# A mixture-of-experts layer and a LoRA layer on one core: the same work in a newly searched order

## The chip, the cores and the metric

The kernel runs on one core of a Trainium2 chip. A core has a matrix engine (TensorE, PE in the profile; its weight loads are PEld), three engines for elementwise work (VectorE or DVE, ScalarE or ACT, GpSimd or POOL) and SyncE (SP), which here only issues DMAs. Each engine works through its own queue in order, and they wait for each other by semaphores. The metric is the device time of one execution in microseconds (us), median of several runs.

## The reference

The input `x` is 2 batch rows x 1024 tokens x 256 channels; `cond_8` (2 x 8) holds the router's logits and also the LoRA weights. Cut to what is computed:

```python
rw = softmax(router_logits); w, sel = top_k(rw, 2); w = w / w.sum()
mlp(x, g, u, d) = (gelu(x @ g) * (x @ u)) @ d          # 256 -> 1024 -> 256
x = x + sum(w[k] * mlp(x, expert sel[k])) + mlp(x, shared)
x = x + x @ W_base.T + b_base + 2.0 * sum_e cond[b, e] * Bs[e] @ (As[e] @ x)
```

The router picks per batch row, so each row runs one shared and two chosen experts. The second line is computed as one matrix per batch row, `W_base` plus the mixed LoRA product.

## The kernel before, in words

**Tiling.** The tokens of a batch row are two tiles `t` of 512, the channels two blocks `c` of 128. Work on the experts goes in 24 *groups* `g` = (batch row, shared or chosen expert 1 or 2, quarter of the 1024 hidden units), 12 per batch row. Every f32 operand is kept as two parts: `hi`, a rounded copy (`hi_of`, a cast by ScalarE, L179), and `lo`, the rest (`lo_of`, a subtraction by VectorE or GpSimd, L182). A product is three matmuls: hi x hi, lo x hi, hi x lo of weights and x, in this order (L289), so the low half of x is wanted by the third.

**A group.** Groups 1 to 23 compute the 2 x 2 block product (hidden half `i`, token tile `j`) with seven products instead of eight, by sums of weight blocks (`weight_sum`, S1 to S4, on GpSimd, L221) and of x blocks (`x_sum`, L261 to L267). They are named P1 to P7, with g or u behind for the gate or the up half: P1, P6, P7 and P4 go into PSUM banks `ps_ag`/`ps_au`, P2, P5 and P3 into `ps_dg`/`ps_du`. On the way ScalarE copies a bank out (`keep`: r1 after P1, u2 after P6, u3 after P7, L316) and VectorE adds the copy to the d bank (`add_part`, named "r1 added u" and so on, L322). Then for each block `ij`: `gelu ij` on ScalarE (L331), `act ij` = `times_up` on VectorE (gelu times up times gate weight, L337/L339), `act_hi` (ScalarE) and `act_lo` (VectorE), and two halves of `down` on TensorE (L361) into four banks `y[j][c]`, which add up over the 12 groups of a batch row. A name with 10 behind it, as `times_up 10`, means block i = 1, j = 0; block 10 reads `ps_ag`/`ps_au` directly, so the next group's P1 has to wait for `gelu 10` and `times_up 10`. Group 0 is computed plainly with eight products (`plain_product`, L311), the first of them in two halves of 256 tokens, as its inputs are just arriving; its block products are called "product ij of k" (k is the half of the 256 channels).

**Order.** There is no scheduler at run time: the program hands each piece of work to `at(t, f, ...)` with a planned time in units of one TensorE product of 0.68 us (`LEN = 22` units a group), the list is sorted by that time, and a dependency chain fixes this order on every engine. Pieces that come in each group get the time `g * LEN + REGULAR[name]` by `reg`. `MOVED` shifts single pieces, named by their place in the list, against their time. So a planned time sets only the order in each queue; what waits at run time is decided by data and buffers. Names in the table: "A hi/A1 lo/A2 lo" split the weight blocks of the next group, "S hi/S lo" the sums, "D hi/D0 lo/D1 lo" the down weights, "load" fetches the weights of the group after next: from HBM by SP for the shared expert, by an indirect DMA on GpSimd's queue for the chosen ones.

**Start, batch change and end.** SP issues the first loads in pieces; 27 small matmuls warm TensorE up. The router runs in group 1 or so (`router`, seven VectorE operations; `gate_exp` and `gelu_table` on ScalarE switch its function table twice). At the end of batch row 0, `finish_y` (L406) adds `y` to the old x and so frees the four `y` banks for the next row's `down`; `split_xa` splits the sum for the second layer, whose two LoRA matrices were made in groups 4 and 5 (`weff_*`). The second layer of row 0 runs beside the other row's end, then that of row 1.

Of the kernel before, what the change touches and what calls it, by code (L numbers as in the profile page):

```python
# [53 lines left out]
SCALING = 2.0  # L54
PIECE = 2
REGULAR = {
    "P1g": -3.9, "P2g": -1.8, "P1u": -0.9, "S1": -0.9, "r1g": -0.8, "A hi": -0.3, "r1 added g": 0.9,
    "r1u": 1.1, "P6g": 2.7, "u2g": 2.7, "P6u": 4.6, "P2u": 5.0, "u2u": 6.0, "S2": 6.7, "P7g": 7.3, "S4": 7.3,
    "P5g": 7.6, "S3": 7.7, "A1 lo": 7.8, "load": 7.9, "u3g": 8.5, "P5g mix": 9.6, "P7u": 10.6,
    "r1 added u": 12.2, "P5u": 12.7, "P4g": 13.2, "u3 added g": 13.3, "gelu 00": 14.1, "act 00": 14.1,  # L60
    "u3u": 14.2, "S hi": 14.8, "P3g": 15.5, "P4u": 15.7, "S lo": 16.0, "gelu 11": 16.0, "gelu 10": 16.1,
    "hi 00": 17.0, "u3 added u": 17.8, "act 11": 18.0, "P3u": 18.1, "u2 added g": 18.1, "act 10": 18.4,
    "hi 11": 18.8, "down 00 0": 19.7, "u2 added u": 20.8, "gelu 01": 20.8, "lo 00": 21.2, "act 01": 23.3,
    "hi 10": 25.6, "lo 10": 25.6, "lo 11": 25.7, "down 00 1": 26.2, "hi 01": 28.6, "down 10 0": 29.0,
    "down 10 1": 31.1, "lo 01": 31.6, "A2 lo": 31.6, "D hi": 34.0, "down 11 0": 34.2, "down 11 1": 34.2,
    "down 01 0": 34.3, "D1 lo": 34.3, "down 01 1": 34.5, "D0 lo": 36.4,
}
MOVED = {
    33: -4.6, 40: 6.9, 59: -0.5, 75: -1.5, 87: -22.6, 100: 1.7, 101: 3.2, 190: 0.2, 1587: 10.8, 1599: 5.5,
    1605: 5.0,  # L70
}
WARM = 27
LEN = 22
# [15 lines left out]
def moe_then_lora(ctx: ExitStack, tc: tile.TileContext, x, cond, skill, shared, piece0, second, outT):  # L89
# [16 lines left out]
    def at(t, f, *args):  # L106
        plan.append((round(t + MOVED.get(len(plan), 0), 1), len(plan), f, args))
# [210 lines left out]
    sums, ge, act, acts = {}, {}, {}, {}  # L318
# [49 lines left out]
    mix, bias_sb = lin[:, (2 + NC) * C:(2 + NC) * C + B], lin[:, (2 + NC) * C + B:]  # L368
# [77 lines left out]
    V, A, G = nc.vector, nc.scalar, nc.gpsimd  # L446
# [50 lines left out]
    for n, ij in enumerate(((0, 0), (1, 0), (0, 1), (1, 1))):  # L497
        t = (6, 8, 10, 16)[n]
# [72 lines left out]
    for g, b in MIX_AT.items():  # L571
        t0 = g * LEN
# [23 lines left out]
    for b in range(B):  # L596
        t0 = (b + 1) * (1 + TOP_K) * NPC * LEN
# [3 lines left out]
    for b in range(B - 1):  # L601
        t0 = (b + 1) * (1 + TOP_K) * NPC * LEN
        for t in range(T):
            for c in range(NC):
                at(t0 + (10.2, 14.2)[t] + c / 10, finish_y, b, t, c)
                at(t0 + (t + 1) * LEN + 8 + 8 * c, split_xa, b, t, c, hi_of, A)
                at(t0 + (t + 1) * LEN + 9 + 8 * c, split_xa, b, t, c, lo_of, V)


    t0, tt = NG * LEN, (NG - 1) * LEN  # L610
    b = B - 1
# [96 lines left out]
```

## Time and profile before

| what | us |
|---|---|
| median of 3 runs (lowest, highest) | 383.69 (383.64, 384.94) |
| the profiled execution's own time | 383.77 |
| its span, first to last instruction | 382.0 |
| TensorE busy | 377.4 |
| VectorE busy | 307.5 |
| ScalarE busy | 255.6 |
| GpSimd busy | 207.6 |
| granted TensorE clock | 1.000 |

Matmuls are pipelined, so that each is shown longer (0.39) than the distance to the next (0.23); lost time on TensorE is best read from starts, not from busy time. In a row of the timeline the columns are start, length, engine, line, operation, what it writes and reads, count of merged instructions, and in brackets the engine's idle time before it with what ended it. A VectorE operation's recorded length overlaps the next one's start by about 0.08.

### The profile page before, as it was taken

The page shows a single profiled execution, that of the slowest core. Times are in us where ns is not written, and L with a number is a line of the kernel's source. Part 1 is how long each engine was busy: PE and PEld are TensorE (multiplying, and loading weights), DVE is VectorE, ACT ScalarE, POOL GpSimd, SP SyncE. Part 2 cuts the span into 40 slices and gives each one's busy share as a digit, 9 for nine tenths or more (in the row PEclk, how much of TensorE's full clock was granted, in tenths as well). Part 3 has the DMA queues.
Part 4 walks back from the last instruction along what each step waited for, and adds up shares of the span by engine and source line. Part 5 has one row for each costly group of instructions (what it writes and reads, how often), then busy time and mean ns, then how long its engine had stood idle before and what let it go on. Part 6 is the DMA issues. An engine that isn't in the chain of part 4 may idle for free.

```text
span 382.0 us, 4888 instructions
## 1 busy us (share of the span) xinstructions
PE 377.4 (99%) x1695; PEld 312.4 (82%) x1695; DVE 307.5 (81%) x423; ACT 255.6 (67%) x439; POOL 207.6 (54%) x215
## 2 busy tenths in 40 slices
PE   9999999999999999999999999999999999999996
PEld 8788788888888888888888888888888888888885
DVE  5999978678787889988798897777778778777686
ACT  3878876776666866867767777667666667665520
POOL 0587777777565574553454655755555556550100
PEclk9999999999999999999999999999999999999999
DMA  8711220220211204041250112012022021000014
GB/s 232 275 46 55 85 82 1 84 82 0 84 29 53 86 5 160 2 137 36 103 192 1 45 41 82 9 75 82 2 82 82 2 84 54 28 2 0 0 57 165
DMA packets 8215, 26.00 MB, mean 68 GB/s; under 512 B 1024, under 2 KB 2304, under 8 KB 8192
## 3 DMA queue, kind: packets, MB, share of 16 engines
q0 software_dynamic: 2304, 12.58, 10.6%
q1 hardware_dynamic: 5888, 13.12, 10.0%
q8 instruction: 13, 0.21, 0.2%
q14 instruction: 10, 0.08, 0.1%
HBM read 23.60 MB, written 2.10 MB: 67 GB/s over the span
## 4 chain that ended last, share of the span: by engine, by line
PE 96%; DMA 1%; DVE 1%; SPq 1%; ACT 0%; issue 0%
PE y L361 34%; PE ps_au L289 17%; PE ps_ag L289 17%; PE ps_dg L289 13%; PE ps_du L289 13%; DMA w_raw<-in_piece 1%; SPq L255 0%; PE ps_dg L384 0%; PE ps_dg L311 0%; PE ps_du L311 0%; SPq L209 0%; DVE wd L182 0%; ACT acts L179 0%; DVE act L337 0%; DVE xr L263 0%
## 5 line engine op out<-in xcount | busy, mean ns | idle before, releaser
L361 PE MATMUL y<-acts,wd 128*128 128x512 f32 x576 | 150.1, 390 | 0.4 <-ACT acts L179 0.4
L361 PEld LDWEIGHTS y<-acts,wd 128*128 128x128 f32 x576 | 107.8, 188 | 23.3 <-ACT acts L179 0.8
L182 DVE TENSOR_TENSOR acts<-act,acts 128x512 fp32r<-128x512 f32 x96 | 76.2, 820 | 14.2 <-ACT acts L179 13.7
L182 POOL TENSOR_TENSOR wa<-w_raw,wa 128x512 fp32r<-128x512 f32 (+1 forms) x46 | 56.1, 1224 | 30.4 <-ACT wa L179 24.0
L182 POOL TENSOR_TENSOR wd<-w_raw,wd 128x256 fp32r<-128x256 f32 x44 | 37.2, 863 | 53.6 <-ACT wd L179 53.5
L221 POOL TENSOR_TENSOR sf<-w_raw 128x256 f32<-128x256 f32 x46 | 37.3, 811 | 49.9 <-DVE ws L182 38.9
L179 ACT CAST acts<-act 128x512 fp32r<-128x512 f32 x96 | 58.0, 620 | 4.7 <-DVE act L337 2.8
L339 DVE SCALAR_TENSOR_TENSOR act<-ge,gate_w,c_u 128x512 f32<-128x512 f32 x48 | 46.5, 970 | 3.0 <-ACT ge L331 0.5
L331 ACT ACTIVATE ge<-c_g 128x512 f32<-128x512 f32 x69 | 43.7, 633 | 0.4
L331 ACT ACTIVATE ge<-ps_ag 128x512 f32<-128x512 f32 x24 | 14.4, 601 | 43.6 <-PE ps_ag L289 43.6
L322 DVE TENSOR_TENSOR c_u<-ps_du,u_u 128x512 f32<-128x512 f32 x46 | 31.6, 686 | 12.0 <-PE ps_du L289 12.0
L182 DVE TENSOR_TENSOR ws<-sf,ws 128x1024 fp32r<-128x1024 f32 (+1 forms) x24 | 28.2, 1179 | 14.7 <-ACT ws L179 14.7
L316 ACT COPY u_g<-ps_ag 128x512 f32<-128x512 f32 x46 | 27.1, 589 | 18.4 <-PE ps_ag L289 16.4
L289 PE MATMUL ps_au<-x,ws 128*128 128x512 f32 x138 | 38.9, 390 | 0.0
L289 PE MATMUL ps_ag<-x,ws 128*128 128x512 f32 x138 | 38.8, 389 | 0.0
L289 PE MATMUL ps_au<-x,wa 128*128 128x512 f32 x138 | 38.8, 389 | 0.0
L289 PE MATMUL ps_ag<-x,wa 128*128 128x512 f32 x138 | 38.7, 389 | 0.0
L289 PE MATMUL ps_du<-x,ws 128*128 128x512 f32 x138 | 38.7, 389 | 0.0
L289 PE MATMUL ps_dg<-x,ws 128*128 128x512 f32 x138 | 38.7, 389 | 0.0
L316 ACT COPY u_u<-ps_au 128x512 f32<-128x512 f32 x46 | 27.0, 588 | 13.4 <-PE ps_au L289 13.4
L322 DVE TENSOR_TENSOR c_g<-ps_dg,u_g 128x512 f32<-128x512 f32 x46 | 31.3, 680 | 5.1 <-PE ps_dg L289 4.7
L289 PEld LDWEIGHTS ps_au<-x,ws 128*128 128x128 f32 x138 | 25.8, 188 | 5.7 <-ACT u_u L316 0.4
(105 smaller groups left out, 554.6 us busy)
## 6 DMA issues: line engine op xcount, KB each, us to landing
w_raw<-in_shared SPq DMA_DIRECT2D x7, 768.0 KB, 4.5
xr<-in_x SPq DMA_DIRECT2D x15, 256.0 KB, 3.6
lora_in<-in_second SPq DMA_DIRECT2D x1, 514.0 KB, 6.1
w_raw<-in_piece SPq DMA_DIRECT2D x4, 128.0 KB, 2.7
outT<-sf SPq DMA_DIRECT2D x1, 512.0 KB, 2.8
outT<-u_g SPq DMA_DIRECT2D x2, 256.0 KB, 2.0
outT<-u_u SPq DMA_DIRECT2D x2, 256.0 KB, 2.0
outT<-ge SPq DMA_DIRECT2D x4, 128.0 KB, 1.7
```

Of the source, the lines that this page charges most:

```text
L179: (eng.copy if eng is nc.scalar else eng.tensor_copy)(pair[:, 0, :], src)
L182: eng.tensor_tensor(pair[:, 1, :], src, pair[:, 0, :].bitcast(F32), ALU.subtract)
L221: eng.tensor_tensor(ssum(i), a, b, op)
L289: nc.tensor.matmul(ps, lhsT=l, rhs=r, start=(start and n == 0), stop=(n == len(parts) - 1), skip_group_check=True)
L316: nc.scalar.copy(part[m, h], bank["a", h])
L322: nc.vector.tensor_tensor(sums[g, h, ij], bank["d", h], part[m, h], ALU.add)
L331: nc.scalar.activation(ge[g, ij], result(g, 0, ij), AF.Gelu_apprx_tanh)
L339: nc.vector.scalar_tensor_tensor(act[g, ij], ge[g, ij], gate_w[:, s - 1, b:b + 1], result(g, 1, ij), ALU.mult, ALU.mult)
L361: nc.tensor.matmul(y[j][c], lhsT=w[:, wp, o:o + P], rhs=a[:, ap, :], start=first and n == 0, stop=last and n == 2, skip_group_check=True)
```

## The change

No instruction is added or taken away; only the planned times are others, and so the order in the queues. Three places change: the table of regular times, the list of moved pieces (11 before, 52 after), and the planned times of `finish_y` for the first batch row. Most of the moved pieces lie in groups 0 to 6 (places 24 to 410). Among them: place 24 is the low split of P2's x block of group 0, 33 an `x_sum`, 37 `gate_weights`, 59 and 78 the `gelu 10` and the `act_lo 11` of group 0, 87 to 101 the sums and their splits for groups 1 and 2, 110 to 198 products, keeps and loads of groups 1 and 2, 1539 the split of the first LoRA matrix, 1557 and 1559 splits of the second batch row's x, 1599 and 1605 splits at the end.

```diff
 REGULAR = {
-    "P1g": -3.9, "P2g": -1.8, "P1u": -0.9, "S1": -0.9, "r1g": -0.8, "A hi": -0.3, "r1 added g": 0.9,
-    "r1u": 1.1, "P6g": 2.7, "u2g": 2.7, "P6u": 4.6, "P2u": 5.0, "u2u": 6.0, "S2": 6.7, "P7g": 7.3, "S4": 7.3,
-    "P5g": 7.6, "S3": 7.7, "A1 lo": 7.8, "load": 7.9, "u3g": 8.5, "P5g mix": 9.6, "P7u": 10.6,
-    "r1 added u": 12.2, "P5u": 12.7, "P4g": 13.2, "u3 added g": 13.3, "gelu 00": 14.1, "act 00": 14.1,
...
-    "hi 10": 25.6, "lo 10": 25.6, "lo 11": 25.7, "down 00 1": 26.2, "hi 01": 28.6, "down 10 0": 29.0,
-    "down 10 1": 31.1, "lo 01": 31.6, "A2 lo": 31.6, "D hi": 34.0, "down 11 0": 34.2, "down 11 1": 34.2,
-    "down 01 0": 34.3, "D1 lo": 34.3, "down 01 1": 34.5, "D0 lo": 36.4,
+    "P1g": -3.7, "S1": -1.3, "r1g": -0.3, "P2g": 0.0, "S2": 0.8, "P1u": 1.2, "A hi": 1.4, "P6g": 1.6,
+    "r1 added g": 1.9, "r1u": 2.2, "load": 3.4, "u2g": 3.8, "S4": 3.8, "P6u": 4.6, "P2u": 5.0, "P7g": 6.5,
+    "u2u": 6.6, "S3": 7.0, "P5g": 7.2, "u3g": 7.2, "gelu 00": 9.7, "P5g mix": 10.1, "r1 added u": 10.3,
+    "P7u": 10.5, "S hi": 10.6, "u3 added g": 11.6, "P5u": 12.0, "A1 lo": 12.1, "u3u": 12.9, "act 00": 13.5,
...
+    "down 00 1": 24.5, "hi 10": 26.0, "lo 11": 28.2, "lo 10": 28.4, "hi 01": 28.7, "down 11 0": 29.4,
+    "down 10 0": 30.1, "D hi": 30.4, "lo 01": 30.8, "A2 lo": 32.5, "down 11 1": 33.6, "D1 lo": 37.8,
+    "down 10 1": 38.6, "down 01 0": 39.1, "D0 lo": 39.2, "down 01 1": 40.1,
 }
 MOVED = {
-    33: -4.6, 40: 6.9, 59: -0.5, 75: -1.5, 87: -22.6, 100: 1.7, 101: 3.2, 190: 0.2, 1587: 10.8, 1599: 5.5,
-    1605: 5.0,
+    24: 3.3, 33: -9.8, 37: 3.8, 45: 3.7, 59: -1.6, 78: 3.8, 87: -35.7, 92: 2.9, 97: 8.9, 99: 6.7, 100: 6.7,
+    101: 5.2, 107: -4.6, 110: -2.1, 111: -0.7, 115: -1.7, 120: -0.9, 121: -3.7, 124: 2.7, 128: -2.9,
...
+    347: -4.2, 349: 4.4, 350: -4.6, 351: 2.5, 355: -8.3, 407: 6.8, 410: -6.4, 780: -0.9, 1539: 7.4,
+    1557: 5.4, 1559: 2.4, 1599: 1.6, 1605: 1.9,
 }
...
-                at(t0 + (10.2, 14.2)[t] + c / 10, finish_y, b, t, c)
+                at(t0 + (16.8, 18.4)[t] + c / 10, finish_y, b, t, c)
```

## The prediction

> **What bounds the kernel now.** I read the busy shares first, then the table by stage, then the chain of waits, and only then single instructions where the chain leaves TensorE.
>
> The page's first two parts (engine, busy time and share; then tenths in 40 slices):
>
> ```profile
> PE 377.4 (99%) x1695; PEld 312.4 (82%) x1695; DVE 307.5 (81%) x423; ACT 255.6 (67%) x439; POOL 207.6 (54%) x215
> PE   9999999999999999999999999999999999999996
> PEclk9999999999999999999999999999999999999999
> ```
>
> TensorE has work in every slice but the last and its clock is full. The busy time of single stretches (start:end, length, then each engine's busy time) says where it isn't:
>
> ```profile
> 0.00:17.00 17.00, 15.81 (x86) 13.10 (x87) 12.01 (x23) 8.79 (x17) 4.50 (x10) 1.00 0.84 277
> 17.00:41.00 24.00, 24.00 (x106) 19.39 (x105) 22.20 (x37) 20.63 (x37) 19.12 (x18) 1.00 0.18 50
> 41.00:189.00 148.00, 148.00 (x660) 122.69 (x659) 122.35 (x161) 105.80 (x182) 93.53 (x96) 1.00 0.20 66
> ```
>
> From 41 us on TensorE is busy every moment. The chain in order of time (start, length, what) shows the pace; one group is what lies between two of these rows:
>
> ```profile
> 101.56 2.72 PE y L361 x12
> ...
> 116.52 2.72 PE y L361 x12
> ...
> 131.48 2.72 PE y L361 x12
> ```
>
> 2.72/12 = 0.2267 us a matmul, 14.96 us = 66 x 0.2267 a group: no slot is lost. No order can shorten that; it can only lose. What an order can win are the slots lost before 41 us. TensorE's instructions in order of time there:
>
> ```profile
> 10.98 1.52 PE L311 MATMUL y<-x,wa 128*128 128x512 f32 x6
> 12.85 1.77 PE L361 MATMUL y<-acts,wd 128*128 128x512 f32 x6 [0.36 <-ACT acts L179]
> 14.46 0.39 PE L311 MATMUL ps_dg<-x,ws 128*128 128x512 f32 x1
> ...
> 18.59 0.94 PE L289 MATMUL ps_dg<-x,wa 128*128 128x512 f32 x3
> 19.37 0.86 PE L361 MATMUL y<-acts,wd 128*128 128x512 f32 x3
> ...
> 38.44 0.84 PE L361 MATMUL y<-acts,wd 128*128 128x512 f32 x3
> 39.21 0.96 PE L289 MATMUL ps_au<-x,ws 128*128 128x512 f32 x3
> 40.01 1.32 PE L361 MATMUL y<-acts,wd 128*128 128x512 f32 x5
> ```
>
> Starts against starts: from 10.98 to 14.46 are 3.48 us for 12 slots of 0.2267 (2.72), so 0.76 lost: group 0's first `down`, which waits for its activations. 18.59 to 19.37 is 0.78 for three slots (0.68): 0.10, P2g of group 1 behind `gelu 11`. 38.44 to 40.01 is 1.57 for six (1.36): 0.21, P7u of group 2 behind `keep u2 u`. With about 0.15 at the first matmul (3.88) that is 1.2 us, all there is to win; the span cannot fall below 382.0 - 1.2 = 380.8, a time of 382.6.
>
> **Outside the change.** SP's queue is in the same order in both kernels, TensorE's first 13 products too, ScalarE's work up to about 17 us, and the tail's products from 362 us (there only the lo splits of the last group and of the last sums change places). So the 3.88 us ahead of the first matmul and the 4.3 us after the last stay: 0.
>
> **Part 1: P2's low half three places later on VectorE (the loads assumed late).** VectorE's rows:
>
> ```profile
> 7.29 0.42 DVE L179 CAST x<-xr 128x512 fp32r<-128x512 f32 x1
> 7.75 0.69 DVE L182 TENSOR_TENSOR x<-xr,x 128x512 fp32r<-128x512 f32 x1
> 8.72 0.43 DVE L182 TENSOR_TENSOR wa<-w_raw,wa 128x256 fp32r<-128x256 f32 x1 [0.27 <-ACT wa L179]
> 9.06 0.68 DVE L263 TENSOR_TENSOR xr<-xr,xr 128x512 f32<-128x512 f32 x1
> 9.66 0.69 DVE L261 TENSOR_TENSOR xr<-xr,xr 128x512 f32<-128x512 f32 x1
> ```
>
> The 7.75 row is P2's low half. In the new order the L263 sum takes its place (to about 8.40), the wa split still starts at 8.72 (it waits for ScalarE, whose cast waits for its load), and P2's low half starts at 9.06 and ends at 9.75. L261 then starts at 9.66 as before: the rest of VectorE's chain (P3, wd, `times_up 00` at 11.47) keeps its times. But TensorE's product 00 of k=1 reads that half in its fifth matmul, at 9.16; it now waits to 9.75 + 0.05 = 9.80 (0.05 is what the `down` at 12.85 took after its cast ended at 12.80). Loss: 0.64. `gelu 00` starts at 10.59 when ScalarE is free, and the accumulation now ends at 9.80 + 0.23 + 0.39 = 10.42: no delay; `gelu 10` moves from 11.08 to about 11.6 and ends before ScalarE's next cast at 12.18. So TensorE arrives at `down 00` at 12.34 + 0.64 = 12.98, after the activations' hi half (12.85); its fifth matmul comes at 12.98 + 0.91 = 13.89, just as the lo half is there (13.16 + 0.68 + 0.05). It ends at 14.34 where it was 14.46. The wait of 0.76 has changed places with one of 0.64: net -0.12.
>
> A rule that would make it dearer: the Trainium skill (VectorE: DVE Perf Modes, The DRAIN you can't avoid) says that the next Vector operation does not start until the pipe is empty; its next section lets an instruction that is not held start earlier. Here 9.06 starts 0.09 before 8.72 + 0.43. By the drain rule P2's low half would end at 9.15 + 0.69 = 9.84, a loss of 0.73 and a net of -0.03. I take the rows.
>
> **Part 2: groups 0 to 2.** P6's low half moves up into VectorE's idle 0.69 us before `act_lo 10` (15.13): 14.36 to 15.05, cost nothing. Against this stands the Trainium skill (GPSIMD Engine Reference, 1. Specifications): GpSimd shares its SBUF interfaces with Vector instructions of two SBUF inputs. GpSimd works from 13.40 to 15.00, and the sum at 12.07, beside GpSimd, took 1.17. At that price `act_lo 10` slips by 0.4; TensorE reads it at about 19.2, nearly 3 us after its end, so the sum stays. P2g goes two products later (about 20.5), `gelu 11` ends about 19.7: the 0.10 goes. In group 2 `keep r1 u` follows a P1u that sits one product later, but `act_hi 10` now stands ahead of the table switch and not behind it: P1u ends about 34.3, the keep 34.95; two table loads (1.28 each) and two 0.20 operations end about 37.9; `keep u2 u` 38.4, P7u wants it at 38.9: the 0.21 goes, with 0.45 to spare. The router's seven operations (2.0 us, 22.64 to 24.66 now) pass `act_lo 11`, which then ends about 25.2; its `down` wants it at 26.9. P5u of group 1 moves two products later and wants `r1 added u` (26.4) at 28.0. Narrowest is `times_up 10` of group 1: at the stretched durations it ends about 33.0, and P1u of group 2, moved one product later, wants it at 33.5. New waits here: 0 to 0.5, taken as 0.05, since all stand at zero with the rows' own durations.
>
> **Part 3: the regular times.** TensorE's products are the same; two other engines' reads of its banks change. The tightest wait every group has is P6u on `keep r1 u` (it ends at 200.79, P6u starts at 201.36: 0.57), and it is untouched. The others, counted in products of 0.68 between a bank's writer and its next use: from P6g to P7g there were five and are four, so P7g's margin on `keep u2 g` goes from 1.93 to 1.25. From P2u to P5u there were ten and are seven, 2.04 less, of which VectorE gives back some, as `r1 added u` also moves up: from about 3.6 to 2.1; in groups 13 and 14, where the second layer's splits stand on VectorE, 0.8. From P4g to the next group's P1u there were seven and are ten: the margin on `times_up 10` grows from 1.7 to about 3. GpSimd's load of two groups ahead is issued 4.5 units (3 us) earlier, ahead of S4 and S3: those come 1.3 us later, some 8 us ahead of their reader. Nothing: 0. If a stretched Vector operation (0.5 more, 12.07 against 9.66) meets a narrow group, 0.5 each; not in all.
>
> **Part 4: the sums at the batch change.** Now:
>
> ```profile
> 190.45 1.29 DVE L406 TENSOR_TENSOR xa<-y,xr 128x512 f32<-128x512 f32 x2 [1.34 <-PE y L361]
> 193.85 0.69 DVE L406 TENSOR_TENSOR xa<-y,xr 128x512 f32<-128x512 f32 x1 [0.32 <-PE y L361]
> ```
>
> All four move behind the last `down` of group 11, which itself is later. That ends about 197.3; two sums of 0.69 (0.60 apart) run to 198.6; behind them on VectorE stands `times_up 10` of group 12 (0.68), to 199.2, and P1u of group 13 needs it at about 199.3 (TensorE now: 199.32). Margin near 0.1; taken as 0.05, at most 0.5, with `act_lo 00` behind it still 0.3 early.
>
> **Sum.** -0.12 - 0.10 - 0.21 + 0.05 + 0.05 = -0.33 on the profiled execution's 383.77 (span 382.0 and 1.77 around it): 383.44. That execution is 0.08 above the median of 383.69, so on the median it is 383.36. I say 383.4.
>
> **Rivals.** (a) The old waits go but new ones of the same size come, in group 1 and at the batch change (0.5 + 0.5 at their upper ends, less what is counted): 383.4 + 0.4 to 0.9, so 383.8 to 384.3. For it: VectorE is busy 22.2 of 24 us between 17 and 41. Against: each wait has a margin at the measured durations. (b) Slower than before by one mechanism: P2's low half is late and `down 00` doesn't absorb it, because its activations slip as far. Place: product 00, k=1, at 9.16; price 0.64 + 0.12 back: 383.4 + 0.76 = 384.2. It decides as soon as L261 starts over 0.4 us after 9.66. Against: the wa split, the load behind it, and P2's low half end where that chain began before. (c) A regular wait in every group: P5u's margin of 2.1 is used up. From 0.1 us in each of 22 groups: 385.6 and more. For it: one operation stretches by 0.5; against: it takes four or five in a row. (d) The change does nothing that counts: 383.7.
>
> **Numbers.** Chances: forecast 0.55 (own range 383.0 to 383.8), (d) 0.12, (a) 0.15, (b) 0.08, (c) 0.08, all idle gone with luck 0.02. Half a per cent, about what a measurement of this kernel can tell from no change, is 1.9 us; below 381.8 lies under the 382.6 that TensorE's work allows. Hence faster 0.02, same 0.90, slower 0.08. Range 382.8 to 384.8, from the floor to past (a) and (b).
>
> **What would show it.** TensorE's fifth matmul of product 00, k=1, starting at 9.8; no wait left at `down 00`, P2g of group 1 or P7u of group 2; the spacing of 14.96 kept; P1u of group 13 with at most 0.2 lost. A spacing above 15.0, or a wait over 1 us anywhere after 17 us, would make it wrong.

## The result and the profile after

| | before | after |
|---|---|---|
| median, us (lowest to highest, runs) | 383.86 (383.60 to 384.94, 22) | 384.87 (384.35 to 385.70, 22) |
| ratio to before, 95% interval | | 1.0021, 1.0015 to 1.0027 |
| the profiled execution's own time | 383.77 | 385.22 |
| its span | 382.0 | 383.4 |
| VectorE busy | 307.5 | 317.4 |

The changed kernel is slower by 0.21% (0.15 to 0.27%), some 0.8 us (the two medians lie 1.0 apart); that is within the half per cent that was called no change. Forecast was 0.3 us less than before, so the sign is wrong, and the time lies just outside the range.

The page's first part, and then the busy time of single stretches (start:end, length, then PE, PEld, DVE, ACT and POOL with their counts, granted clock, DMA share, GB/s), both of the kernel after:

```profile
PE 377.6 (98%) x1695; PEld 312.3 (81%) x1695; DVE 317.4 (83%) x423; ACT 254.4 (66%) x439; POOL 204.4 (53%) x215
```

```profile
0.00:17.00 17.00, 15.10 (x84) 12.75 (x85) 12.07 (x23) 8.71 (x16) 3.97 (x9) 1.00 0.80 268
17.00:41.00 24.00, 24.00 (x108) 19.77 (x107) 20.31 (x36) 21.05 (x38) 18.20 (x18) 1.00 0.26 85
41.00:189.00 148.00, 147.43 (x656) 121.70 (x655) 129.60 (x162) 104.24 (x182) 95.19 (x97) 1.00 0.18 61
189.00:205.00 16.00, 16.00 (x72) 13.19 (x71) 14.23 (x21) 10.83 (x20) 6.93 (x8) 1.00 0.34 116
205.00:355.00 150.00, 150.00 (x664) 124.19 (x663) 121.58 (x156) 101.51 (x175) 78.18 (x83) 1.00 0.13 43
```

Three things are to be seen. From 205 to 355 us, some ten groups, TensorE is busy every moment, and its starts there keep the pace of 0.2267 us without a loss: the new regular times cost nothing in each group. Around the batch change (189 to 205) it is full too. But between 41 and 189, where it was full before, 0.57 us are missing, and VectorE took 129.6 us where it took 122.4, for one operation more. So VectorE's operations became longer there, not more.

Read as in the prediction (starts against starts), TensorE's lost slots are these, in us, each with the 0.11 or so that the matmul after a wait comes late as well:

| place | before | after |
|---|---|---|
| the first product, from 3.88 to 5.51 us | 0.27 | 0.27 |
| product 00 of k=1, on P2's low half | 0 | 1.33 |
| first `down` 00 of group 0 | 0.74 | 0 |
| P2g of group 1, P7u of group 2 | 0.29 | 0 |
| P2g of group 3 | 0 | 0.11 |
| **P5g of group 4** | 0 | **0.85** |
| `down` 11 of group 23 | 0 | 0.11 |
| second layer at the end | 0.15 | 0.15 |
| sum | 1.45 | 2.82 |

The difference is 1.37; the spans differ by 1.44, the rest being remnants below 0.04 each. The start has 0.6 of it, and P5g of group 4 has 0.85; the small waits gone (0.29) and come (0.22) nearly cancel. The timeline of after shows what happened at the start:

```profile
8.86 0.41 ACT L183 CAST wa<-w_raw 128x256 fp32r<-128x256 f32 x1 [2.54 <-DMA w_raw<-in_piece]
...
9.30 0.43 DVE L186 TENSOR_TENSOR wa<-w_raw,wa 128x256 fp32r<-128x256 f32 x1 [1.12 <-ACT wa L183]
...
9.64 0.68 DVE L186 TENSOR_TENSOR x<-xr,x 128x512 fp32r<-128x512 f32 x1
...
10.38 0.50 PE L315 MATMUL ps_ag<-x,wa 128*128 128x512 f32 x1 [1.06 <-DVE x L186]
...
13.69 1.52 PE L365 MATMUL y<-acts,wd 128*128 128x512 f32 x6
```

In this execution the fourth weight piece landed 0.58 us later than in the one of before (ScalarE's cast, 8.86 against 8.28), and everything behind it moved by as much: the `wa` split from 8.72 to 9.30, P2's low half to 9.64, the matmul to 10.38. `down` 00 (13.69) no longer waits.

The other part is P5g of group 4. The same view of after, 64 to 71 us:

```profile
64.31 0.75 POOL L225 TENSOR_TENSOR sf<-w_raw,sf 128x256 f32<-128x256 f32 x1
64.39 3.84 DVE L341 TENSOR_TENSOR act<-ge,c_u 128x512 f32<-128x512 f32 x1
...
65.01 0.73 POOL L186 TENSOR_TENSOR wa<-w_raw,wa 128x256 fp32r<-128x256 f32 x1
...
65.70 0.73 POOL L225 TENSOR_TENSOR sf<-w_raw 128x256 f32<-128x256 f32 x1
...
66.40 1.28 POOL L186 TENSOR_TENSOR wa<-w_raw,wa 128x512 fp32r<-128x512 f32 x1
...
68.27 0.62 ACT L183 CAST acts<-act 128x512 fp32r<-128x512 f32 x1 [1.25 <-DVE act L341]
68.79 0.58 ACT L320 COPY u_g<-ps_ag 128x512 f32<-128x512 f32 x1
69.28 0.62 ACT L183 CAST wd<-w_raw 128x512 fp32r<-128x512 f32 x1
69.79 0.59 ACT L393 COPY wef<-ps_dg 128x512 f32<-128x512 f32 x1
...
70.43 0.96 PE L293 MATMUL ps_dg<-x,ws 128*128 128x512 f32 x3 [0.57 <-ACT wef L393]
```

From below upwards: P5g needs the bank `ps_dg`, out of which ScalarE must first copy the LoRA product (`weff_keep`, L393). That copy is the third in ScalarE's queue behind a cast of `act` (68.27), for which ScalarE stood idle for 1.25 us. The `act` is VectorE's `times_up 01` of group 3, and that took 3.84 us where such an operation, with no GpSimd beside it, takes 0.68. While it lasted, GpSimd worked through four operations without a break (64.31 to 67.68): S4, the A2 split of group 4, S3 and the A1 split of group 5. `times_up` ended 0.55 after the last of them. In the kernel before, the same pieces lay far apart:

```profile
60.20 1.07 POOL L221 TENSOR_TENSOR sf<-w_raw,sf 128x256 f32<-128x256 f32 x1
61.22 0.74 POOL L221 TENSOR_TENSOR sf<-w_raw 128x256 f32<-128x256 f32 x1
...
63.41 1.29 POOL L182 TENSOR_TENSOR wa<-w_raw,wa 128x512 fp32r<-128x512 f32 x1 [1.44 <-ACT wa L179]
...
64.05 1.20 DVE L337 TENSOR_TENSOR act<-ge,c_u 128x512 f32<-128x512 f32 x1
...
69.42 0.73 POOL L182 TENSOR_TENSOR wa<-w_raw,wa 128x256 fp32r<-128x256 f32 x1
```

S4 and S3 (60.20, 61.22) were done before `times_up 01` began, A2 (69.42) stood behind the LoRA sum, and `times_up` met A1 alone: 1.20 us, ended again 0.55 after it. Two changes made the row. The new regular times put the load ahead of S4 and S3 and so bring these two beside `times_up` (`b_regular` below, which has the new times without the new list, has them at 64.35 and 65.06 us and lost nothing at P5g); the moves of places 230 and 292 by -3.9 and -4.7 put the two splits there too.

### The profile page after: what moved, and what is told of

It reads as the page before. It is cut to its first block, busy times and chain, and to the rows that moved or that the text cites. A ratio compares the mean times of both kernels' runs of the same rounds, so it can differ in the third digit from the quotient of the medians.

```text
span 383.4 us, 4919 instructions
## 1 busy us (share of the span) xinstructions
PE 377.6 (98%) x1695; PEld 312.3 (81%) x1695; DVE 317.4 (83%) x423; ACT 254.4 (66%) x439; POOL 204.4 (53%) x215
## 4 chain that ended last, share of the span: by engine, by line
PE 95%; DVE 1%; DMA 1%; SPq 1%; ACT 1%; issue 0%; DVEq 0%
PE y L365 34%; PE ps_au L293 17%; PE ps_ag L293 17%; PE ps_dg L293 13%; PE ps_du L293 13%; DMA w_raw<-in_piece 1%; DVE act L341 1%; PE ps_du L315 1%; PE ps_dg L315 1%; SPq L259 0%; PE y L315 0%; SPq L213 0%; PE ps_dg L388 0%; ACT acts L183 0%; DVE x L186 0%
## 5 line engine op out<-in xcount | busy, mean ns | idle before, releaser
L365 PE MATMUL y<-acts,wd 128*128 128x512 f32 x576 | 156.9, 389 | 0.0
L186 DVE TENSOR_TENSOR acts<-act,acts 128x512 fp32r<-128x512 f32 x96 | 72.9, 780 | 5.3 <-ACT acts L183 5.0
L186 POOL TENSOR_TENSOR wd<-w_raw,wd 128x256 fp32r<-128x256 f32 x44 | 39.4, 913 | 69.0 <-ACT wd L183 69.0
L186 POOL TENSOR_TENSOR wa<-w_raw,wa 128x512 fp32r<-128x512 f32 (+1 forms) x46 | 53.7, 1168 | 29.3 <-ACT wa L183 29.2
L225 POOL TENSOR_TENSOR sf<-w_raw 128x256 f32<-128x256 f32 x46 | 38.3, 832 | 37.9 <-DVE ws L186 26.7
L343 DVE SCALAR_TENSOR_TENSOR act<-ge,gate_w,c_u 128x512 f32<-128x512 f32 x48 | 52.2, 1088 | 1.9 <-ACT ge L335 0.5
L320 ACT COPY r_g<-ps_ag 128x512 f32<-128x512 f32 x23 | 13.5, 587 | 45.6 <-PE ps_ag L293 45.6
L186 DVE TENSOR_TENSOR ws<-sf,ws 128x1024 fp32r<-128x1024 f32 (+1 forms) x24 | 33.0, 1380 | 1.6 <-ACT ws L183 0.2
L326 DVE TENSOR_TENSOR c_g<-ps_dg,r_g 128x512 f32<-128x512 f32 x23 | 15.9, 690 | 22.2 <-PE ps_dg L293 22.2
```

Source lines behind the costliest of these rows:

```text
L186: eng.tensor_tensor(pair[:, 1, :], src, pair[:, 0, :].bitcast(F32), ALU.subtract)
L225: eng.tensor_tensor(ssum(i), a, b, op)
L320: nc.scalar.copy(part[m, h], bank["a", h])
L326: nc.vector.tensor_tensor(sums[g, h, ij], bank["d", h], part[m, h], ALU.add)
L343: nc.vector.scalar_tensor_tensor(act[g, ij], ge[g, ij], gate_w[:, s - 1, b:b + 1], result(g, 1, ij), ALU.mult, ALU.mult)
L365: nc.tensor.matmul(y[j][c], lhsT=w[:, wp, o:o + P], rhs=a[:, ap, :], start=first and n == 0, stop=last and n == 2, skip_group_check=True)
```

## The experiments

The theories, as the expectations name them: **A**, the low half of P2 that was moved costs the time. **B**, the order at the start is neutral; the fourth piece's landing decides, and the wait only changes its place. **C**, GpSimd's row of four holds `times_up 01` of group 3, and through it `weff_keep` and P5g of group 4. **D**, the new regular times cost something in each group. Of `MOVED` an edit shows only the part of a line that changes.

### The low half of P2, back and alone

In the changed kernel, P2's low half back at its old place (`a_p2_back`):

```diff
-    24: 3.3, 33: -9.8, 37: 3.8, 45: 3.7,
+    33: -4.6, 37: 3.8, 45: 3.7,
```

> The changed kernel with one thing undone: P2's low half of group 0 stands again right behind its cast on VectorE, ahead of the x sum and the wa split. Theory A (the moved low half costs time by itself): TensorE's fifth matmul of product 00, k=1, starts again at about 9.2 and not at 10.4; the wait moves back to the first down, but smaller; time 384.87 - 0.57 = 384.3. Theory B (in both orders VectorE's chain hangs on the wa split, and so on the landing of the fourth weight piece; the place of the low half only moves the wait): the loss at product 00 goes, the loss at the first down comes back as 0.76 us plus whatever the piece lands later than 8.25; time within 0.15 of 384.87. Theory C (GpSimd's four operations in a row in group 3 make the loss): no change either, and the wait of 0.85 at P5g of group 4 stays.

In the kernel before, the moved low half alone (`b_p2_late`):

```diff
-    33: -4.6, 40: 6.9,
+    24: 3.3, 33: -9.8, 40: 6.9,
```

> The kernel before with the low half of P2 alone moved behind the x sum and the wa split, as in the changed kernel. Theory A: 383.86 + 0.57 = 384.4. Theory B: within 0.15 of 383.86; a loss of 0.6 us or more at product 00, k=1, takes the place of the loss of 0.76 or more at the first down. C says nothing of it: 383.9.

Measured: `a_p2_back` 385.12 us, ratio to before 1.0030 (1.0017 to 1.0043), so nothing was given back. `b_p2_late` 384.35, ratio 1.0007 (0.9995 to 1.0019): no cost that can be told from none, but the 0.57 us of A (0.15%) lie in this interval too. The timeline of `a_p2_back`:

```profile
8.28 0.41 ACT L183 CAST wa<-w_raw 128x256 fp32r<-128x256 f32 x1 [1.53 <-DMA w_raw<-in_piece]
...
12.86 1.82 PE L365 MATMUL y<-acts,wd 128*128 128x512 f32 x6
...
69.97 0.98 PE L293 MATMUL ps_dg<-x,ws 128*128 128x512 f32 x3 [0.58 <-ACT wef L393]
```

Here the piece landed as early as before, product 00 lost nothing, and a small wait is at `down` 00 again (1.82 for six matmuls instead of 1.52). P5g of group 4 still waits. A falls by this kernel, whose interval lies above A's 384.3; B and C stand. `b_p2_late` says less than was hoped: in its profiled execution TensorE's first matmuls were slow (last section), so it came to product 00 after the low half was ready and lost nothing there, and `down` 00 lost its 0.74 all the same, behind a piece that landed at 11.01 us instead of 10.04.

### GpSimd's row of operations

Three edits of the changed kernel act on the chain at different links. `a_train2` takes both moved splits out of the row, `a_train3` only one, and `a_keep` leaves the row as it is and puts the copy one place forward in ScalarE's queue, ahead of the cast of the down weight:

```diff
# a_train2
-    198: 1.2, 224: -5.6, 230: -3.9, 267: 2.5, 292: -4.7,
+    198: 1.2, 224: -5.6, 267: 2.5,
# a_train3
-    198: 1.2, 224: -5.6, 230: -3.9, 267: 2.5, 292: -4.7,
+    198: 1.2, 224: -5.6, 267: 2.5, 292: -4.7,
# a_keep
-    1557: 5.4, 1559: 2.4,
+    1536: -0.2, 1557: 5.4, 1559: 2.4,
```

> The changed kernel with two entries of the moved list taken out: GpSimd's two low splits (A2 of group 4, A1 of group 5) go back behind the first LoRA sum, so that VectorE's times_up 01 of group 3 meets two GpSimd operations in a row (S4, S3) and not four. Theory C: that operation takes about 0.55 us beyond the end of the second one, some 2.0 us instead of 3.84, the keep of the LoRA product leaves ScalarE in time, P5g of group 4 waits no more (0.85 saved), time 384.87 - 0.85 = 384.0. Theory A or B alone (the loss is at the start): 384.9, the wait at the start unchanged. A regular loss in every group: 384.9.

> The changed kernel with only the A2 split of group 4 put back, so that times_up 01 of group 3 meets three GpSimd operations in a row (S4, S3, A1). Theory C, that a Vector operation with two SBUF inputs is let in only where GpSimd leaves a gap: it ends 0.55 after the third, so about 0.75 shorter than 3.84, near 3.1; P5g of group 4 then waits 0.1 or not at all: 384.87 - 0.75 = 384.1. If it shared the port in turns with GpSimd, its length would not follow the row, and the time would stay at 384.9.

> The changed kernel with one exchange on ScalarE: the copy of the LoRA product of group 4 (weff_keep, L393) goes ahead of the cast of the down weight (D hi) that stands in front of it. GpSimd's row of four operations and VectorE's order are untouched. Theory C (the row of four holds times_up 01 of group 3, ScalarE's cast of act waits for it, and the copy queues behind): times_up still takes 3.8 us, but the copy starts at about 69.3 instead of 69.8, so P5g of group 4 loses about 0.25 + 0.11 instead of 0.74 + 0.11 and the time falls by 0.5 against the changed kernel: about 384.4. If the wait at P5g were due to something on TensorE or to the bank itself: 0.74 stays lost, 384.9.

| kernel | GpSimd's row, operations | `times_up 01` of group 3, us | lost at P5g of group 4, us | median, us | ratio to before (95%) |
|---|---|---|---|---|---|
| after | 4 | 3.84 | 0.74 + 0.11 | 384.87 | 1.0021 (1.0015 to 1.0027) |
| `a_keep` | 4 | 3.84 | 0.23 + 0.11 | 384.38 | 1.0010 (1.0003 to 1.0017) |
| `a_train3` | 3 | 3.15 | 0.05 + 0.11 | 384.39 | 1.0005 (0.9995 to 1.0015) |
| `a_train2` | 2 | 1.22 | 0 | 384.13 | 1.0001 (0.9992 to 1.0010) |

The medians come from different rounds, so kernels are best compared by the ratios. The timelines at this place, `a_train2` first, then `a_keep`:

```profile
63.90 0.76 POOL L225 TENSOR_TENSOR sf<-w_raw,sf 128x256 f32<-128x256 f32 x1
63.99 1.22 DVE L341 TENSOR_TENSOR act<-ge,c_u 128x512 f32<-128x512 f32 x1
64.60 1.20 POOL L225 TENSOR_TENSOR sf<-w_raw 128x256 f32<-128x256 f32 x1
...
68.39 0.59 ACT L393 COPY wef<-ps_dg 128x512 f32<-128x512 f32 x1
```

```profile
63.59 3.84 DVE L341 TENSOR_TENSOR act<-ge,c_u 128x512 f32<-128x512 f32 x1
...
68.47 0.59 ACT L393 COPY wef<-ps_dg 128x512 f32<-128x512 f32 x1
68.95 0.63 ACT L183 CAST wd<-w_raw 128x512 fp32r<-128x512 f32 x1
69.11 0.98 PE L293 MATMUL ps_dg<-x,ws 128*128 128x512 f32 x3
```

With the row cut to two, `times_up` ends at 65.21, 0.55 after the first of them and not after the second as expected (1.22 us instead of 2.0), and now it is GpSimd's second operation that is stretched (1.20 for 0.73). The loss is gone, and with it the whole difference to the kernel before that can be measured. `a_keep` shows the lower end of the chain: the operation is as long as ever, but the copy passes one cast of 0.5, and P5g loses 0.5 less, as expected to 0.02 us. That what matters is the place in ScalarE's queue, and not the bank or TensorE, is thereby shown. The length of `times_up` follows the row (3.84, 3.15, 1.22 for four, three, two operations), and the loss at P5g follows it. C holds, link by link.

### Both undone, and an attempt at something better

`a_both` joins the edits of `a_p2_back` and `a_train2`. `a_best` keeps P2's low half directly behind its cast, takes the two splits out of the row, and moves four more pieces against the small waits that were left:

```diff
-    24: 3.3, 33: -9.8, 37: 3.8,
+    24: 0.25, 33: -9.8, 37: 3.8,
-    224: -5.6, 230: -3.9, 267: 2.5, 292: -4.7,
+    224: -5.6, 267: 2.5,
-    1557: 5.4, 1559: 2.4,
+    183: -1.0, 1515: -2.7, 1536: -0.2, 1544: -0.2, 1557: 5.4, 1559: 2.4,
```

> Both undone at once. Theory A and C together: 384.87 - 0.57 - 0.85 = 383.45, below the kernel before. B and C: 384.0, as the kernel with the GpSimd order alone. If neither accounts for the loss: 384.9.

> The changed kernel with GpSimd's row cut to two, P2's low half of group 0 back behind its cast but the x sum still ahead of the wa split (so that the sum no longer waits for the fourth weight piece), and four pieces moved so that the small waits of 0.11 us go: add_part u2 g of group 2 ahead of times_up 11, the copies of the LoRA products ahead of the cast of the down weights, and act_lo 11 of the last group ahead of the second store. Theory B and C: -0.85 for the row, -0.3 for the small waits, and L261 follows at once on the wa split, 0.6 earlier on VectorE where the load is late, -0.2 to -0.6 at the start: 384.87 - 1.35 to 1.75 = 383.1 to 383.5, below the kernel before by 0.5. If the start hangs on something else: 383.7.

`a_both`: 384.26, ratio 1.0008 (0.9999 to 1.0017), nearer to B and C (384.0) than to A and C (383.45). `a_best`: 384.09, ratio 1.0000 (0.9990 to 1.0011), a miss: the waits at P2g of group 3, at P5g of groups 4 and 5 and in group 23 are gone, but P5u of group 5 now loses 0.19 + 0.11 and `down` 00 0.37. What an order can still win here is of the size of what the start varies by (last section), and no kernel of the study is shown to beat the one before.

### The new regular times without the moved pieces

The kernel before with the changed kernel's table of regular times and its times for the sums, but its own list of moved pieces, less the one that moved a sum (`b_regular`); and the same with the two splits pulled forward (`b_regular_train`):

```diff
# b_regular: REGULAR and the times of finish_y as in the changed kernel, and
-    190: 0.2, 1587: 10.8, 1599: 5.5,
+    190: 0.2, 1599: 5.5,
# b_regular_train, besides
-    33: -4.6, 40: 6.9,
+    230: -3.9, 292: -4.7, 33: -4.6, 40: 6.9,
```

> The kernel before with the new regular times and the new times of the batch row's sums (which the later downs need), but with its own 11 moved pieces less the one that these sums replace. Theory C (the loss sits in the moved pieces: GpSimd's row of four in group 3): GpSimd's order there is S4, S3 and then the LoRA sum, times_up 01 of group 3 takes about 2.0 us, P5g of group 4 does not wait by 0.8; time about that of the kernel before, 384.0, within 0.5. Theory D (the regular times cost in every group): 0.04 us or more in each of 22 groups, 384.9 and more.

> The same with two of the new moved pieces alone: the low splits A2 of group 4 and A1 of group 5 moved up behind S4 and S3 on GpSimd. Theory C: the row of four is there again, times_up 01 of group 3 takes about 3.8 us, P5g of group 4 waits 0.75 to 0.85: 0.8 over the kernel with the regular times alone. Any other theory: the same as that one.

Both expectations missed. `b_regular` took 387.43 us, ratio 1.0097 (1.0084 to 1.0110): far more than C said, and not in the way that D meant. The loss is not in each group; it is at single places in groups 1 to 6, each the end of a buffer or bank chain. The two largest that lie on a row of GpSimd, in its timeline:

```profile
35.13 3.80 DVE L337 TENSOR_TENSOR act<-ge,c_u 128x512 f32<-128x512 f32 x1
...
41.87 0.96 PE L289 MATMUL ps_du<-x,ws 128*128 128x512 f32 x3 [0.29 <-DVE c_u L322]
...
97.80 6.16 DVE L182 TENSOR_TENSOR acts<-act,acts 128x512 fp32r<-128x512 f32 x3
...
104.62 0.97 PE L289 MATMUL ps_du<-x,ws 128*128 128x512 f32 x3 [0.78 <-DVE c_u L322]
```

`times_up 01` of group 1 takes 3.80 us beside a row of four, and P5u of group 2 loses 0.45 + 0.11; three `act_lo` of group 5 take 6.16 us where they would take 1.9 (0.68 + 2 x 0.60), the first two 1.22 each beside one GpSimd operation, the third 3.71 beside a row of four, and P5u of group 6 loses 0.94 + 0.11. (For P5u of group 2 the router's operations stand in VectorE's queue between the two as well, so that the row's share of that loss isn't shown.) So the long list of moved pieces is what makes the new table bearable. The list with the old table was not run.

`b_regular_train` took 386.92, ratio 1.0082 (1.0069 to 1.0095), and not 0.8 more: P5g of group 4 lost nothing.

```profile
65.39 0.74 POOL L182 TENSOR_TENSOR wa<-w_raw,wa 128x256 fp32r<-128x256 f32 x1
65.48 0.84 PE L289 MATMUL ps_ag<-x,ws 128*128 128x512 f32 x3
65.68 2.95 DVE L337 TENSOR_TENSOR act<-ge,c_u 128x512 f32<-128x512 f32 x1
...
70.19 0.59 ACT L389 COPY wef<-ps_dg 128x512 f32<-128x512 f32 x1
```

The row of four is there, but VectorE, held back by TensorE's earlier losses, came to it when its second operation was running, and so sat through three. The copy was in time. What a row costs depends on which of its operations is met, and a shift of 0.8 us elsewhere is enough to change that.

### The sums at the batch change alone

The kernel before with the four sums at their new times (`b_sums`), and then also with `act_lo 00` of group 12 one place ahead on VectorE (`b_sums_lo`):

```diff
# b_sums
-    190: 0.2, 1587: 10.8, 1599: 5.5,
+    190: 0.2, 1599: 5.5,
...
-                at(t0 + (10.2, 14.2)[t] + c / 10, finish_y, b, t, c)
+                at(t0 + (16.8, 18.4)[t] + c / 10, finish_y, b, t, c)
# b_sums_lo, besides
-    190: 0.2, 1599: 5.5,
+    190: 0.2, 830: -0.5, 1599: 5.5,
```

> The kernel before with one part of the change alone: the four sums at the change of batch row at the new times, behind the last down of group 11. The prediction's part 4: margin 0.1 at P1u of group 13, so 0 to 0.2 lost near 199 us, time within 0.2 of the kernel before. Rival (a): 0.5 lost there or at the first activations of group 12, 0.5 slower.

> The kernel before with the four sums at their new times, and one exchange on VectorE: act_lo 00 of group 12 goes ahead of the add of u2 and u, behind the last sum. In the run with the sums alone act_lo started at 200.30, 0.30 after GpSimd's wa split began (200.00), took 1.54 us and ended at 201.84, 0.55 after that split's first operation, and the fifth matmul of down 00 lost 0.75 + 0.11. If the stretch by GpSimd is the cause (C carried to this place): act_lo now starts at about 199.7, ahead of GpSimd, takes 0.7 to 1.0, nothing is lost, and the time is that of the kernel before (within 0.2). If the sums as such are too dear on VectorE here: act_lo moves up by 0.6 only, so 0.15 + 0.11 stay lost and the add behind it makes something else late, 0.3 or more slower.

`b_sums` took 384.91, ratio 1.0026 (1.0016 to 1.0035): alone, the part that costs nothing in the changed kernel costs 0.9 us. `b_sums_lo` took 383.83, ratio 0.9996 (0.9983 to 1.0008): one exchange takes it all back. The timelines of `b_sums`, of `b_sums_lo` and of the changed kernel there:

```profile
198.51 1.28 DVE L406 TENSOR_TENSOR xa<-y,xr 128x512 f32<-128x512 f32 x2
...
200.00 2.44 POOL L182 TENSOR_TENSOR wa<-w_raw,wa 128x512 fp32r<-128x512 f32 x2 [2.01 <-ACT wa L179]
...
200.30 1.54 DVE L182 TENSOR_TENSOR acts<-act,acts 128x512 fp32r<-128x512 f32 x1
...
201.90 0.73 PE L361 MATMUL y<-acts,wd 128*128 128x512 f32 x2 [0.59 <-DVE acts L182]
```

```profile
199.30 0.67 DVE L182 TENSOR_TENSOR acts<-act,acts 128x512 fp32r<-128x512 f32 x1
199.59 2.77 POOL L182 TENSOR_TENSOR wa<-w_raw,wa 128x512 fp32r<-128x512 f32 x2 [2.01 <-ACT wa L179]
```

```profile
200.85 0.68 DVE L186 TENSOR_TENSOR acts<-act,acts 128x512 fp32r<-128x512 f32 x1
...
201.28 1.41 POOL L186 TENSOR_TENSOR wa<-w_raw,wa 128x512 fp32r<-128x512 f32 x1 [2.82 <-ACT wa L183]
```

In `b_sums` the `act_lo` starts 0.30 after GpSimd's split and takes 1.54, and a `down` loses 0.75 + 0.11. In `b_sums_lo` it starts 0.29 ahead of the split and takes 0.67. In the changed kernel ScalarE's cast of these weights ("A hi", -0.3 before and 1.4 after) stands later in the queue, so GpSimd's split begins 0.43 after `act_lo`: the new regular times are what pays for the moved sums. `b_regular`, which has these two parts of the change and not the list, bears it out: the same 0.43, and no loss from 189 to 205. It is the mechanism of C at another place, with a row of two.

The sums at their old times in the changed kernel weren't tried: they would stand ahead of the last `down` of group 11 and so compute something else.

## Why the prediction was wrong

- **Outside the change, 0.** The queues' order was as said. The start was not the same in the two profiled executions, because a load landed 0.58 later; that is no work of the change.
- **Part 1, -0.12.** The mechanism is right, and with the landing added its numbers are the measured ones: start of P2's low half 9.06 + 0.58 = 9.64 (9.64), the fifth matmul 9.80 + 0.58 = 10.38 (10.38), loss 0.64 + 0.58 = 1.22 (1.22), and the wait at `down` 00 gone. One term is missing: the matmul after the wait came 0.11 late as well, which was counted in the 0.76 at `down` 00 (0.52 and twice 0.11) but not in the 0.64. With it the exchange comes to 0 and not -0.12. What the step took as fixed, the start of the `wa` split at 8.72, hangs on a load. In the runs the sign can't be told: alone the move gave +0.07% (-0.05 to 0.19%).
- **Part 2, waits of groups 0 to 2.** The waits at P2g of group 1 and P7u of group 2 are gone, and no new one came in these groups. But the step ended at group 2, and the list of moved pieces goes on to place 410. The moves of GpSimd's splits for groups 4 and 5 (230 and 292) were given no price at all, nor was P2g of group 3, which lost 0.11.
- **Part 3 is the step that failed**: "those come 1.3 us later, some 8 us ahead of their reader. Nothing: 0. If a stretched Vector operation (0.5 more, 12.07 against 9.66) meets a narrow group, 0.5 each". It asked of S4 and S3 only whether they come in time for their reader, not which Vector operation they would meet; in group 4 they came some 4 us later (60.20 and 61.22 before, 64.31 and 65.70 after), right beside `times_up 01`. And its stretch, taken from one row, was that of a single GpSimd operation. The real one was 3.16 us more (3.84 against 0.68; it was 1.20 in the kernel before), because with the two splits that Part 2 left out GpSimd had four operations behind one another; one group was narrow, and it cost 0.85. That no wait came in every group and the spacing of TensorE kept was right.
- **Part 4, 0.05.** Nothing was lost, but for a reason that the step had not named: without the new place of the weights' cast the same sums lose 0.86.
- **The sum.** -0.29 for the two waits gone, +0.85 at P5g, +0.11 in group 3 and +0.11 in group 23 give +0.78 with the start neutral; measured is 0.8 (0.6 to 1.0).

The Trainium skill (GPSIMD Engine Reference, 1. Specifications), which the prediction weighed at one place only and found harmless there, states just this contention: the SBUF interfaces of GpSimd are shared with Vector instructions of two SBUF inputs. The skill's page SBUF — State Buffer (SBUF: two separate sides) says that the shared pair is locked for a whole instruction and that the other side blocks fully. The rows agree (`times_up` of the kernel before waited one GpSimd operation out, 1.20 us), and go further: the waiting operation isn't always let in after one instruction (3.84 us over four). Of the rivals, (a) came nearest in kind, new waits in place of the old, but in group 4, where it had not looked; (b) and (c) are refuted by `a_p2_back` and by the full stretch from 205 to 355.

## What to carry to other kernels

Where VectorE reads two SBUF operands while GpSimd works, price the operation by the row of GpSimd's operations that it can meet, at most to the end of the last and 0.55 us more, not by one of them; then follow who is queued behind its reader on the other engines. Go through a list of moved pieces to its end and look at every place where a move puts GpSimd's operations next to each other. An order that was searched as a whole can't be priced part by part: two of its parts here each cost 0.9 us or more alone that other parts had paid for.

## What the runs showed of the hardware

**A Vector operation with two SBUF inputs can be held over several GpSimd operations.** In all the rows looked at here the stretched operation ended 0.55 to 0.56 us after the end of some GpSimd operation, but of which one varied: the first of two (`a_train2`, `b_sums`), the third of three (`a_train3`), the fourth of four (after, `a_p2_back`, `a_keep`, `b_regular`), once the third of four (`a_train2` at 79.70 us, 3.11 us long). What decides it is open: `a_train2` and `a_train3` have the same first two operations (S4, S3) at the same distance, and only the former's `times_up` was let in after the first. Vector operations that read a PSUM bank were not touched: adds and `times_up` from PSUM beside GpSimd's work took 0.68 to 0.69 (after, 59.70 and 60.99 us).

**A load's landing varies between executions.** The fourth weight piece landed at 8.25 us in the profiled execution of before, at 8.84 in that of after, and between 7.25 (`b_regular`) and 9.14 (`a_train3`) in the others. These are different kernels, but it was issued at 4.00 us in all.

**TensorE's first matmuls are slow in some executions.** They then ran at nearly half the pace, in spite of 27 small ones ahead of them; the granted clock reads 1.00 in both kinds of execution, so the cause isn't shown. Two neighbouring rows of the kernel before, then of `b_sums_lo`:

```profile
5.03 0.28 PE L311 MATMUL ps_ag<-x,wa 128*128 128x256 f32 x1
5.15 0.28 PE L311 MATMUL ps_au<-x,wa 128*128 128x256 f32 x1
```

```profile
5.13 0.41 PE L311 MATMUL ps_au<-x,wa 128*128 128x256 f32 x1
5.34 0.41 PE L311 MATMUL ps_ag<-x,wa 128*128 128x256 f32 x1
```

The distance is 0.12 in the one and 0.21 in the other, up to about 5.7 us there, 6.1 us in `b_p2_late` and 6.3 us in `a_both`: up to 1 us lost, part of which then falls into waits that are there anyway. It and the landing are of the size of the whole effect that was looked for, which is why differences of 0.3 us between single kernels of the study say nothing.
